# Moving two one-hot builds ahead of the block statistics on VectorE, and the square root behind a copy on ScalarE, in a one-core graph layer

## The chip, the cores and the metric

The kernel runs on one core of one Trainium2 chip. The metric is the device time of one launch in microseconds: the median of three runs before the change is 260.56 us (260.49 to 260.68).

## The reference

One layer of a graph network over 12,500 nodes (128 features) and 412,500 edges (48 features), sorted by destination node:

```python
h = jnp.maximum(_layernorm(x, axis=-1), 0.0)              # 12500 x 128
agg = jax.ops.segment_sum(edges, recv, num_segments=N)    # edges 412500 x 48, recv = dst, sorted
u = graph_globals[batch]                                  # batch is all zero: one row of 64
z = jnp.concatenate([h, agg, u], axis=1)                  # 240 wide
out = x + relu(z @ W1 + b1) @ W2 + b2                     # hidden width 256
```

Everything is float32.

## The kernel before

The nodes are taken in 12 turns of 1024, counted from 0 here (and a rest of 212 in an epilogue). A turn has two blocks, A and B, of 512 nodes, and 33,792 edges in 11 groups of 3072. The groups lie in six slots: `SLOTS = [(1, 6), (2, 7), (3, 8), (4, 9), (5,), (10, 11)]`; slot 4 holds one group, the others two. The edges of a group come by one DMA of 576 KB; block A and block B of x come by one DMA of 256 KB each. The outputs of the first 11 turns are held on chip (`hold`) and stored after the loop.

What a turn does, by engine. Each engine has its own instruction stream, in the order in which `body(it)` lists the calls, which is written out by hand; `Flow` only derives the semaphore waits from what each step reads and writes.

- **TensorE**, in this order. The sums of the six slots (`su0` to `su5`, L801): edges times one-hot matrices, which add the edges of each short run of nodes. The placing of the sums into the node columns (`place`, L823, and `place_ends`, L785, called `pc5` in the list of steps): sums times wider one-hots ("windows", L751). Second layer of block A of the turn before (`w20`, L907, 16 matmuls), most of the second layer of B (`w21a`, L901), transposes of the normalised blocks (`tu0`, `tu1`, L866), the rest of B's second layer, and the first layer (L876 on the normalised x, L881 on the placed sums).
- **VectorE**. Statistics of block A (`stats`, L831), two small steps (`farthest`, L692 and L694), the fetch of the destination offsets of the next turn (`fetch`, L730, writes `rel_i`), statistics of block B (L831), four small steps to the variance (`variance`, L836 to L841), the one-hot of slot 0 for the next turn (`onehots`, L745), the reciprocal and the shift (`shift`, L850 and L851), the one-hots of slots 1, 2 and 3, the output of block A (`second`, L911, `holda`, from `w20`'s result), the next `xb` of A (L861), one-hots of slots 4 and 5, the same two steps for block B, and the windows.
- **ScalarE**. A copy of each slot's sums out of PSUM (`ss0` to `ss5`, L805), the square root (`root`, L845), the normalisation of the two blocks, four activations each (`norm`, L857; it needs the shift), copies of the placed sums (L872), issue of the DMA that loads the next block A (behind L861 of A), copies of the transposes (L867), issue of the DMA that loads the next block B (behind L861 of B), and the four activations of the first layer (L886).
- **SyncE** issues the edge loads; a group's buffer is loaded again when its slot's sums are done.

Three dependences across engines matter here. `pc5` works in pairs: its first matmul takes the ends kept from the turn before (`ssf`), its second takes `ss5`, and only the weight load of the second waits for ScalarE's copy `ss5` (`late={"ss5": 1}`). L911 `holda` waits for the last matmul of `w20`, which stands right behind `pc5` on TensorE. The one-hot of a slot may be overwritten when this turn's sums of that slot are done, and it reads `rel_i`, which L730 has just written on the same engine.

In `Flow.run`, TensorE's share of a turn has a stretch that is skipped in the first turn (`f.brief = ("w20", "w21a")`). Its branch blocks are named `brief`, `whole` and `both`.

Of the kernel before, what the change touches and what calls it, by code (L numbers as in the profile page):

```python
# [54 lines left out]
class Flow:  # L55
# [14 lines left out]
    def op(self, eng, name, reads, writes, emit, dma=False, late=None):  # L70
        self.seq.append(dict(eng=eng, name=name, r=tuple(reads), w=tuple(writes), emit=emit, dma=dma, it=self.at, late=late or {}))
# [119 lines left out]
    def run(self):  # L191
# [22 lines left out]
        def ahead(e, late=False):  # L214
            for n, c in sorted(self.ahead[e].items()):
                if (e == "PE" and n in self.weights) == late:
                    self.of[e].wait_ge(self.sem[n], (self.rank[n, c] + self.extra[n]) * self.unit(n))

        def repeat(o, i):
            waits = []  # L220
            for n, back in self.body.get(o["name"], []):
                u = self.unit(n)
                waits.append((n, self.sem[n], regs[(o["eng"], u, (self.at_lo[n] - lo - back + self.extra[n]) * u)]))
            self.emit(o, waits, i)
# [26 lines left out]
        pe = nc.tensor  # L251
        blocks = {}

        def part(name, over, come=True):

            if come:
                pe.br("pe_" + name)
            blocks[name] = nc.switch_bb("pe_" + name, parent=over and blocks[over])

        def either(under, yes, no):  # L260

            pe.br_lt(j, under, on_true="pe_" + yes, on_false="pe_" + no)

        n = 4
# [35 lines left out]
        at = "first"  # L300
        for brief, some in groupby(own[:cut], lambda o: o["name"] in self.brief):
            some = list(some)
            if not brief:
                for o in some:
                    if o["name"] in self.stops:
                        stop = "at_" + o["name"]
                        at = "go_" + o["name"]
                        above, under, to = over[stop]
                        part(stop, above)
                        either(under, to, at)  # L310
                        part(at, stop, False)
                    repeat(o, None)
                continue
            either(n + 1, "brief", "whole")
            part("brief", at, False)
            ahead("PE", True)
            for o in some:
                if o["name"] in self.sem:
                    pe.sem_inc(self.sem[o["name"]], 1)
            pe.br("pe_both")  # L320
            part("whole", at, False)
            for o in some:
                repeat(o, None)
            part("both", at)
        pe.br("pe_head")
        part("after", "gate2", False)
        self.straight(end)
# [151 lines left out]
def kernel(  # L479
# [112 lines left out]
    A, B, Z = 0, 1, 2  # L592
# [22 lines left out]
    def load_e(s, j, only=None):  # L615

        for k, g in enumerate(SLOTS[s]):
            if only not in (None, k):
                continue
            dma("SP", f"le{s}.{k}", [], [f"e{s}.{k}"], e[s][:, k * CG:(k + 1) * CG],  # L620
                lambda i, g=g: span(edge_attr, i, lambda i: (i + j) % NIT * IE + g * GE, GE).rearrange("(c p t) d -> p c (t d)", p=P, t=T))
# [68 lines left out]
    def farthest():  # L690

        op("DVE", "fa", ["rel_i"], ["far"], lambda i: [nc.vector.tensor_reduce(  # L692
            far, rel_i.rearrange("p g t -> p (g t)"), AX.X, OP.max, apply_absolute_value=True)])
        op("DVE", "fm", ["far"], ["farm"], lambda i: [nc.vector.tensor_tensor(farm, farm, far, OP.max)])  # L694
# [26 lines left out]
    def fetch(j):  # L721

        it = (f.at or 0) + j
        g0, g1 = it * GI + 1, min(NG, (it + 1) * GI + 1)
        m = GI * CG
        blocks = [b for b in range(NB) if b * P < g1 * CG and (b + 1) * P > g0 * CG]
        rv = rel_i.rearrange("p g (c t) -> p (g c) t", t=T)
        at = lambda i: ((i + j) * GI + 1) * CG

        op("DVE", "fr", ["relz"] + [f"rel{b}.{t0}" for b in blocks for t0 in (0, 3)], ["rel_i"], lambda i: [nc.vector.tensor_scalar(  # L730
            rv, (rel[:, :, at(i):at(i) + m] if isinstance(i, int) else rel[:, :, ds(at(i), m)]).rearrange("p t c -> p c t"),
            0.0, None, OP.add)])
# [8 lines left out]
    def onehot(name, o, reads, r):  # L741

        k, n = r.shape[1], r.shape[2]
        ov = o.rearrange("p (k n) v -> p k n v", k=k)
        op("DVE", f"oh{name}", reads + ["iota_v"], [f"oh{name}"], lambda i: [nc.vector.tensor_tensor(  # L745
            ov, iota_v[:, None, None, :].to_broadcast([P, k, n, V]), r[:, :, :, None].to_broadcast([P, k, n, V]), OP.is_equal)])
# [6 lines left out]
    def onehots(s):  # L753
        g = SLOTS[s]
        onehot(s, oh[s], ["rel_i"], rel_i[:, g[0] - 1:g[0]] if len(g) == 1 else rel_i[:, g[0] - 1:g[1]:g[1] - g[0]])
# [32 lines left out]
    def keep_ends():  # L788
        op("ACT", "ssf", ["ss5"], ["ssf"], lambda i: [nc.scalar.copy(ssf, ss[5])])
# [17 lines left out]
    def sums(s):  # L807
        m = len(SLOTS[s])
        add_up(s, s % 2, oh[s], e[s], ss[s], [f"e{s}.{j}" for j in range(m)], m * CG, {1: (10, 36), 2: (36,)}.get(s, ()))
# [19 lines left out]
    def stats(k, m=P):  # L829
        c = k % 2 * R  # L830
        op("DVE", f"st{k}", [f"x{k}", f"x{k}t"], [f"st{k}"], lambda i: [nc.vector.bn_stats(st[k // 2][:m, c + r], xt[k][:m, r]) for r in range(RR[k])])  # L831

    def variance(n, ks, m=P):
        s, v = sm[n][:m], st[n][:m]
        op("DVE", f"sm{n}.0", [f"st{k}" for k in ks], [f"sm{n}a"], lambda i: [
            nc.vector.tensor_tensor(s[:, 0:2], v[:, :, 1:3].rearrange("p r c -> p c r"), v[:, :, 4:6].rearrange("p r c -> p c r"), OP.add)])  # L836
        op("DVE", f"sm{n}.1", [f"st{k}" for k in ks], [f"sm{n}b"], lambda i: [
            nc.vector.tensor_tensor(s[:, 2], v[:, :, 1], v[:, :, 4], OP.subtract)])
        f.chain("DVE", f"sm{n}.2", [f"sm{n}a"], [f"sm{n}b"],
            lambda: nc.vector.tensor_tensor(s[:, 2], s[:, 2], s[:, 2], OP.mult),  # L840
            lambda: nc.vector.scalar_tensor_tensor(s[:, 3], s[:, 2], D / 4.0, s[:, 1], OP.mult, OP.add))  # L841

    def root(n, m=P):
        op("ACT", f"sq{n}", [f"sm{n}b", "eps"], [f"sc{n}"], lambda i: [
            nc.scalar.activation(sc[n][:m], sm[n][:m, 3], AF.Sqrt, bias=eps[:m], scale=1.0 / D)])  # L845
# [7 lines left out]
    def norm(k, some, m=P):  # L853
        n, c = k // 2, k % 2 * R
        for r in some:
            op("ACT", f"xn{k}.{r}", [f"x{k}", f"x{k}t", f"sc{n}", f"sh{n}"], [f"xn{k}"], lambda i, r=r: [
                nc.scalar.activation(xn[k][:m, r], xt[k][:m, r], AF.Relu, bias=sh[n][:m, c + r:c + r + 1], scale=sc[n][:m, c + r:c + r + 1])])  # L857
# [145 lines left out]
    def body(it):  # L1003
        f.at = it

        def add_slots(*some):
            for s in some:
                sums(s)
                if it < NIT - 1:
                    load_e(s, 1)  # L1010

        keep = lambda i: (i + NIT - 2) % (NIT - 1)
        add_slots(0, 1)
        stats(A)
        farthest()
        fetch(1)
        add_slots(2)
        stats(B)
        variance(0, (A, B))
        root(0)  # L1020
        onehots(0)
        add_slots(3)
        shift(0)
        norm(A, (0,))
        add_slots(4)
        norm(A, (1, 2))
        onehots(1)
        add_slots(5)
        norm(A, (3,))
        norm(B, range(R))  # L1030
        onehots(2)
        onehots(3)
        place(0, (0, 1))
        for s in (1, 2, 3, 4):
            place(s)
        place_ends((0, 1))
        second(A, P, ph[A], "PH0", keep)
        add_b(A)
        for s in (4, 5):
            onehots(s)  # L1040
        second_begun(B, ph[B], "PH1", R - 1)
        sums_out(A)
        sums_out(B)
        if it < NIT - 1:
            load_x(A, lambda i: (i + 1) % NIT * IN)
        turn(A)
        turn(B, P, po, "PO")
        second(B, P, ph[B], "PH1", keep, R - 1)
        add_b(B)
        keep_ends()  # L1050
        if it < NIT - 1:
            load_x(B, lambda i: (i + 1) % NIT * IN + BN)
        places_far()
        fetch_off(1)
        for s in (0, 1, 2, 3, 4):
            places(s)
        places_near()
        layers(layer_x)
        layers(layer_e)
        layers(relu)  # L1060
# [93 lines left out]
```

## Time and profile before

| | us |
|---|---|
| median of 3 runs | 260.56 |
| the profiled execution | 260.67 |
| span of its trace, first to last instruction | 258.9 |
| TensorE matmul busy | 238.8 (92%) |
| VectorE busy | 230.8 (89%) |
| ScalarE busy | 127.9 (49%) |
| HBM rate over the span | 364 GB/s |

Times in the trace are counted from the start of the span. The first turns run while the pipeline of loads fills; the sums of turn 2 start at 62.34 us and those of the last turn at 224.92 us, so that a turn takes about 18.06 us. In a row of the timeline the first number is the start, the second the duration; "x3" merges three instructions, and a bracket tells how long the engine was idle before and what ended it. Rows of the chain of waits and of the list of waits name an engine, the tile that it writes and the line.

### The profile page before, as it was taken

What the parts mean: (1) busy time and instruction counts of PE and PEld (TensorE: products, weight loads), DVE (VectorE), ACT (ScalarE), POOL (GpSimd) and SP (SyncE); (2) the same over time, 40 slices, a digit from 0 to 9 for tenths busy, and PEclk for the clock granted to TensorE, in tenths of its full rate; (3) what the DMA queues carried; (4) which work ended last, traced back from release to release, by engine and by line L of the source; (5) the groups of instructions that cost most, each with busy time, mean ns of one, the idle gap of its engine ahead of it and who ended that gap; (6) DMA issues with size and microseconds to landing.
All of it is one profiled execution on the core that took longest, in us unless ns stands there. A gap on an engine that the chain in (4) does not pass through costs nothing.

```text
span 258.9 us, 17101 instructions
## 1 busy us (share of the span) xinstructions
PE 238.8 (92%) x7539; PEld 188.7 (73%) x7540; DVE 230.8 (89%) x572; ACT 127.9 (49%) x315; POOL 5.2 (2%) x18
## 2 busy tenths in 40 slices
PE   1866699899999999999999999999999999999990
PEld 1766565885976968949949869779589499598680
DVE  6699998978998998998998989989989989989740
ACT  5510273553644725725835646447257358355520
POOL 5000000000000000000000000000000000002000
PEclk9967579999999999999999999999999999999999
DMA  6999999999999999999999999999999999969951
GB/s 189 339 385 388 364 387 392 390 390 393 377 392 389 389 392 387 390 392 384 390 394 385 390 393 386 392 386 385 391 383 390 391 389 390 394 230 363 366 208 65
DMA packets 79508, 94.33 MB, mean 364 GB/s; under 512 B 3227, under 2 KB 72797, under 8 KB 79494
## 3 DMA queue, kind: packets, MB, share of 16 engines
q1 hardware_dynamic: 76086, 88.06, 95.5%
q10 hardware_dynamic: 3312, 6.03, 6.1%
q8 instruction: 7, 0.11, 0.2%
q0 software_dynamic: 96, 0.07, 0.1%
q14 instruction: 7, 0.06, 0.1%
HBM read 87.75 MB, written 6.40 MB: 364 GB/s over the span
## 4 chain that ended last, share of the span: by engine, by line
PE 78%; SPq 14%; DMA 4%; issue 1%; DVE 0%
PE s L801 23%; SPq L597 14%; PE ph L907 12%; PE ph L876 7%; PE ax L823 6%; PE ph L901 6%; PE pt L881 4%; PE pt L876 4%; DMA e<-in_edge_attr_dram 4%; PE ph L881 4%; PE po L876 4%; PE pt L866 2%; PE po L866 2%; PE ax L785 1%; PE ay L785 1%
## 5 line engine op out<-in xcount | busy, mean ns | idle before, releaser
L745 DVE TENSOR_TENSOR oh<-iota_v,rel_i 128x1344 f32<-128x1344 f32 (+1 forms) x78 | 108.7, 1435 | 0.0
L801 PEld LDWEIGHTS s<-e,oh 128*28 128x28 f32 x6336 | 74.2, 111 | 16.8 <-issue 14.5
L801 PE MATMUL s<-e,oh 128*28 128x48 f32 x6336 | 76.9, 212 | 7.4 <-issue 3.5
L886 ACT ACTIVATE hida<-pt,bias 128x512 f32<-128x512 f32 x12 | 8.2, 687 | 50.2 <-PE pt L881 50.2
L857 ACT ACTIVATE xna<-xa,shab,scab 128x128 f32<-128x128 f32 x48 | 23.7, 493 | 13.0 <-DVE shab L851 12.6
L805 ACT COPY ss<-s 128x96 f32<-128x96 f32 (+1 forms) x72 | 16.5, 229 | 26.5 <-PE s L801 25.7
L751 DVE TENSOR_SCALAR pl<-iota_w,off_i 128x186 f32<-128x186 f32 x117 | 27.6, 311 | 0.4
L907 PE MATMUL ph<-w,hida 128*128 128x128 f32 x192 | 24.6, 281 | 0.0
L857 ACT ACTIVATE xnb<-xb,shab,scab 128x128 f32<-128x128 f32 x48 | 23.5, 490 | 1.2
L907 PEld LDWEIGHTS ph<-w,hida 128*128 128x128 f32 x192 | 22.3, 191 | 0.6
L823 PE MATMUL ay<-pl,ss 128*48 128x186 f32 (+1 forms) x120 | 20.9, 324 | 0.0
L823 PE MATMUL ax<-pl,ss 128*48 128x186 f32 (+1 forms) x120 | 20.9, 324 | 0.0
L823 PEld LDWEIGHTS ax<-pl,ss 128*48 128x48 f32 x120 | 14.5, 129 | 4.1
L831 DVE BATCH_NORM_STATS2 stab<-xb 128x6 f32<-128x128 f32 x48 | 10.5, 282 | 6.9 <-DMA xb<-in_x_dram 6.9
L901 PE MATMUL ph<-w,hidb 128*128 128x128 f32 x132 | 16.5, 275 | 0.0
L901 PEld LDWEIGHTS ph<-w,hidb 128*128 128x128 f32 x132 | 15.6, 192 | 0.0
L823 PEld LDWEIGHTS ay<-pl,ss 128*48 128x48 f32 x120 | 14.5, 129 | 0.0
L876 PE MATMUL pt<-hta,w1h 128*128 128x512 f32 x24 | 13.5, 643 | 0.4 <-ACT hta L867 0.4
L881 PE MATMUL po<-ags,w1a 48*128 48x512 f32 x24 | 13.5, 641 | 0.0
L881 PE MATMUL pt<-ags,w1a 48*128 48x512 f32 x24 | 13.5, 641 | 0.0
L867 ACT COPY hta<-pt 128x512 f32<-128x512 f32 x12 | 7.0, 586 | 12.2 <-PE pt L866 12.2
L881 PE MATMUL ph<-ags,w1a 48*128 48x512 f32 x48 | 12.3, 589 | 0.0
(151 smaller groups left out, 330.3 us busy)
## 6 DMA issues: line engine op xcount, KB each, us to landing
e<-in_edge_attr_dram SPq DMA_DIRECT2D x133, 576.0 KB, 8.7
xa<-in_x_dram ACTq DMA_DIRECT2D x11, 256.0 KB, 5.4
xb<-in_x_dram ACTq DMA_DIRECT2D x11, 256.0 KB, 5.4
out_dram<-holda SPq DMA_DIRECT2D x11, 256.0 KB, 3.1
out_dram<-holdb SPq DMA_DIRECT2D x11, 256.0 KB, 3.1
holda<-in_dst_dram SPq DMA_DIRECT2D x4, 384.0 KB, 5.6
e<-in_edge_attr_dram SPq DMA_DIRECT2D x1, 720.0 KB, 4.7
xa<-in_x_dram SPq DMA_DIRECT2D x1, 256.0 KB, 6.6
```

The costliest lines, as they stand in the source:

```text
L597: return [f.of[eng].dma_start(dst_ap(i) if callable(dst_ap) else dst_ap, src_ap(i) if callable(src_ap) else src_ap)]
L745: op("DVE", f"oh{name}", reads + ["iota_v"], [f"oh{name}"], lambda i: [nc.vector.tensor_tensor(ov, iota_v[:, None, None, :].to_broadcast([ ...
L751: nc.vector.tensor_scalar(out[:, j], iota_w, o[j], None, OP.is_equal) for j in range(len(o))])
L801: nc.tensor.matmul(S[k][NV * c:NV * c + V, j * DE:(j + 1) * DE], o[:, (j * CG + c) * T + t], ev[:, j * CG + c, t * DE:(t + 1) * DE], start ...
L805: op("ACT", f"ss{name}", [f"S{k}"], [f"ss{name}"], lambda i: [nc.scalar.copy(sv.rearrange("p j d -> p (j d)"), S[k][:, :m * DE])])
L823: out.append(nc.tensor.matmul(agg[bk][h:h + DE, at:at + w], sv[:, j], pv[:, j, frm:frm + w], start=bk in fresh and bk not in seen, stop=Tr ...
L831: op("DVE", f"st{k}", [f"x{k}", f"x{k}t"], [f"st{k}"], lambda i: [nc.vector.bn_stats(st[k // 2][:m, c + r], xt[k][:m, r]) for r in range(R ...
L857: nc.scalar.activation(xn[k][:m, r], xt[k][:m, r], AF.Relu, bias=sh[n][:m, c + r:c + r + 1], scale=sc[n][:m, c + r:c + r + 1])])
L876: nc.tensor.matmul(o, w1h[:, a * P:(a + 1) * P], hT[k][:, :, :m], start=first, stop=False, skip_group_check=True)])
L881: nc.tensor.matmul(o, w1a[h:h + DE, a * P:(a + 1) * P], ag[k // 2][h:h + DE, :, :m], start=False, stop=True, skip_group_check=True)])
L901: nc.tensor.matmul(ov[:, r], hid[k][:, a, r], w2[:, a], start=(a == 0), stop=(a == NH - 1)) for r in range(n) for a in range(NH)])
L907: nc.tensor.matmul(ov[:m, r], hid[k][:, a, r, :m], w2[:, a], start=(a == 0), stop=(a == NH - 1)) for r in range(begun, RR[k]) for a in ran ...
```

## The change

VectorE builds the one-hot of slot 0 right behind the fetch, ahead of block B's statistics, and that of slot 1 right behind the variance, ahead of the shift. On ScalarE the square root moves behind the copy of slot 3; the first activation of block A moves behind the copy of slot 4, so that in front of the copy of slot 5 there are two activations of block A (three before) and behind it two (one before). TensorE's and SyncE's orders are the same. In `Flow.run` the names of the branch blocks get the name of the step that begins the stretch, so that there could be more than one such stretch; `f.brief` is not changed, and its two steps stand next to each other.

```diff
--- before.py
+++ after.py
@@ -311,17 +311,20 @@
-            either(n + 1, "brief", "whole")
-            part("brief", at, False)
-            ahead("PE", True)
+            tag = some[0]["name"]
+            either(n + 1, "brief_" + tag, "whole_" + tag)
+            part("brief_" + tag, at, False)
+            if tag == self.brief[0]:
+                ahead("PE", True)
...
-            pe.br("pe_both")
-            part("whole", at, False)
+            pe.br("pe_both_" + tag)
+            part("whole_" + tag, at, False)
             for o in some:
                 repeat(o, None)
-            part("both", at)
+            part("both_" + tag, at)
+            at = "both_" + tag
@@ -1014,19 +1017,18 @@
         stats(A)
         farthest()
         fetch(1)
+        onehots(0)
         add_slots(2)
         stats(B)
         variance(0, (A, B))
+        onehots(1)
+        add_slots(3)
         root(0)
-        onehots(0)
-        add_slots(3)
         shift(0)
-        norm(A, (0,))
         add_slots(4)
-        norm(A, (1, 2))
-        onehots(1)
+        norm(A, (0, 1))
         add_slots(5)
-        norm(A, (3,))
+        norm(A, (2, 3))
         norm(B, range(R))
         onehots(2)
         onehots(3)
```

## The prediction

> **What bounds the kernel now.** I read the stretches of single turns first, then the list of waits over turns 2 to 11, then the timelines of VectorE, ScalarE and TensorE side by side in one turn. One turn as a stretch (columns: TensorE, its weight loads, VectorE, ScalarE, GpSimd, then granted clock, DMA share and GB/s), two rows of the list of waits from 60 to 235 us, and the load of block B among the page's DMA issues:
>
> ```profile
> 200.98:219.06 18.08, 18.08 (x614) 14.20 (x614) 17.14 (x43) 9.77 (x25) 0.00 (x0) 1.00 1.08 391
> ```
> ```profile
> DVE stab L831 <- DMA xb<-in_x_dram: 6.2, 10, 0.7
> ACT xna L857 <- DVE shab L851: 11.0, 10, 1.1
> ```
> ```profile
> xb<-in_x_dram ACTq DMA_DIRECT2D x11, 256.0 KB, 5.4
> ```
>
> TensorE looks full (its ends are modelled), the DMA engines look full, and VectorE works 17.14 of 18.08 us. The list names one regular hole of VectorE, 0.6 us per turn for block B of x (5.4 us from issue to landing), and one of ScalarE, 1.1 us for the shift. So I followed turn 2, VectorE first:
>
> ```profile
> 54.26 0.69 DVE L911 TENSOR_TENSOR holda<-ph,xba 128x512 f32 x1 [1.65 <-PE ph L907]
> 58.55 0.69 DVE L861 TENSOR_TENSOR xbb<-xb,b_sb 128x512 f32<-128x512 f32 x1
> ...
> 63.62 0.41 DVE L730 TENSOR_SCALAR rel_i<-rel 128x264 f32 x1
> 64.74 0.87 DVE L831 BATCH_NORM_STATS2 stab<-xb 128x6 f32<-128x128 f32 x4 [0.71 <-DMA xb<-in_x_dram]
> ...
> 66.15 0.17 DVE L841 SCALAR_TENSOR_TENSOR smab<-smab 128x8 f32<-128x8 f32 x1
> 66.24 1.55 DVE L745 TENSOR_TENSOR oh<-iota_v,rel_i 128x1344 f32<-128x1344 f32 x1
> 67.70 0.20 DVE L850 RECIPROCAL scab<-scab 128x8 f32<-128x8 f32 x1
> 67.94 0.17 DVE L851 SCALAR_TENSOR_TENSOR shab<-smab,scab 128x8 f32<-128x8 f32 x1
> 68.02 4.49 DVE L745 TENSOR_TENSOR oh<-iota_v,rel_i 128x1344 f32<-128x1344 f32 x3
> 72.43 0.68 DVE L911 TENSOR_TENSOR holda<-ph,xba 128x512 f32 x1
> ```
>
> VectorE runs without a hole from the statistics of B at 64.74 to the last row and on to L861 of B. ScalarE in the same turn:
>
> ```profile
> 64.70 0.24 ACT L805 COPY ss<-s 128x96 f32<-128x96 f32 x1 [0.56 <-PE s L801]
> 65.73 0.24 ACT L805 COPY ss<-s 128x96 f32<-128x96 f32 x1 [0.79 <-PE s L801]
> 66.35 0.30 ACT L845 ACTIVATE scab<-smab,eps 128x8 f32<-128x8 f32 x1 [0.38 <-DVE smab L841]
> 66.75 0.24 ACT L805 COPY ss<-s 128x96 f32<-128x96 f32 x1
> 68.14 0.49 ACT L857 ACTIVATE xna<-xa,shab,scab 128x128 f32<-128x128 f32 x1 [1.15 <-DVE shab L851]
> 68.54 0.18 ACT L805 COPY ss<-s 128x48 f32<-128x48 f32 x1
> 68.67 1.02 ACT L857 ACTIVATE xna<-xa,shab,scab 128x128 f32<-128x128 f32 x2
> 69.59 0.22 ACT L805 COPY ss<-s 128x96 f32<-128x96 f32 x1
> ...
> 70.12 2.06 ACT L857 ACTIVATE xnb<-xb,shab,scab 128x128 f32<-128x128 f32 x4
> ```
>
> Third, TensorE's weight loads around `pc5`, in turn 1 and in turn 2, with the matmuls of `w20` behind them:
>
> ```profile
> 51.67 0.12 PEld L785 LDWEIGHTS ax<-plf,ssf 128*48 128x48 f32 x1
> 51.68 0.12 PEld L785 LDWEIGHTS ay<-pln,ss 128*48 128x48 f32 x1
> ```
> ```profile
> 69.62 0.20 PEld L785 LDWEIGHTS ax<-plf,ssf 128*48 128x48 f32 x2
> 69.86 0.12 PEld L785 LDWEIGHTS ay<-pln,ss 128*48 128x48 f32 x1
> ```
> ```profile
> 52.17 2.05 PE L907 MATMUL ph<-w,hida 128*128 128x128 f32 x16
> 70.32 2.05 PE L907 MATMUL ph<-w,hida 128*128 128x128 f32 x16
> ```
>
> In turn 1 the load that takes `ss5` follows 0.01 us behind its partner. In turn 2 it comes 0.24 us behind, 0.05 us after the copy `ss5` ends (69.59 + 0.22 = 69.81). No idle time is booked, because earlier matmuls are still drawn as running, but TensorE is held here. So the turn is not set by TensorE's work: it is set by a ring of steps. The shift ends at 68.11; three activations and a copy lie between it and the end of `ss5`; `w20` ends 2.56 us behind `ss5` (70.32 + 2.05 = 72.37); VectorE comes to `holda` at 72.43, 0.06 us behind `w20`. Both ways from the shift to `holda` are equally long, and the ring closes through L861 of B, which ends at 59.24, its load (5.4 us) and the statistics at 64.74.
>
> **The change part by part: the ring with the new order.** I start from `holda` and walk to the next `holda`.
>
> (a) `holda` to the fetch L730: 63.62 − 54.26 = 9.36 us, all of it VectorE's own work, as before. (b) The one-hot of slot 0 now follows the fetch and reads what it wrote. The trace has that pair in the prologue:
>
> ```profile
> 12.94 0.38 DVE L730 TENSOR_SCALAR rel_i<-rel 128x264 f32<-128x264 f32 x1
> 13.35 3.03 DVE L745 TENSOR_TENSOR oh<-iota_v,rel_i 128x1344 f32<-128x1344 f32 x2
> ```
>
> It starts 0.03 us after the fetch ends; with the loop's 0.41 us that is 0.44 us. Its other condition, that the sums of slot 0 are done, holds by then: `ss1` waits for its sums until 64.70 and `ss2` until 65.73, so a slot takes 1.03 us and slot 0 is done by about 63.67; the one-hot starts at 64.06. (c) One-hot of slot 0 to the statistics of B: 1.47 us, the spacing of the row of three, (4.49 − 1.55) / 2. Block B has landed: in the old order it did so at 64.74, and the statistics now begin at 65.53, so the hole of 0.71 us goes. (d) Statistics and variance to the next one-hot: 66.24 − 64.74 = 1.50 us. (e) One-hot of slot 1 to the reciprocal: 1.47 us; its buffer is free, since slot 1's sums end near 64.70 and it starts at 67.03. (f) Reciprocal to the end of the shift: 67.94 + 0.17 − 67.70 = 0.41 us.
>
> So the fetch to the shift's end takes 0.44 + 1.47 + 1.50 + 1.47 + 0.41 = 5.29 us, where it took 68.11 − 63.62 = 4.49 us. The hole paid for only half of the second one-hot: the shift comes 0.80 us later.
>
> The root stays hidden: the variance ends 66.15 + 0.17 − 64.74 = 1.58 us behind the start of B's statistics, so at 67.11, and the copy `ss3`, now ahead of the root, at 66.75 + 0.24 = 66.99; the root takes 0.30 us, and the reciprocal comes only at 68.50. If that cover were gone, up to 0.30 us would join the ring. The copy `ss4` (half a slot, so ready near 67.3) now stands ahead of the first activation and falls into the wait for the shift.
>
> (g) Shift to the first activation: 68.14 − 68.11 = 0.03 us. (h) First to second activation: 1.02 − 0.49 = 0.53 us. (i) Second activation to the copy `ss5`: 0.40 us, as from the activation at 68.14 to the copy at 68.54, and 0.22 us of copy. From the shift to the end of `ss5` that is 1.18 us, where it was 69.81 − 68.11 = 1.70. The edit on ScalarE gives back 0.52 us of the 0.80.
>
> (j) End of `ss5` to the end of `w20`: 2.56 us. (k) End of `w20` to `holda` when VectorE is waiting: 0.04 us, as in turn 1 (52.17 + 2.05 = 54.22 to 54.26). VectorE is waiting now: it has two one-hots behind the shift instead of three, so it is ready 4.32 − 1.47 = 2.85 us after the shift, and `w20` ends 1.18 + 2.56 = 3.74 us after it. The hole that was closed at the statistics opens again at `holda`, about 0.9 us wide.
>
> The ring: 9.36 + 5.29 + 1.18 + 2.56 + 0.04 = 18.43 us. The rows are rounded; 18.41 from the steadier ones (9.35 and 0.40 in the later turns). Before, from turn 2 to the last turn:
>
> ```profile
> 234.94 0.68 DVE L911 TENSOR_TENSOR holda<-ph,xba 128x512 f32 x1
> ```
>
> (234.94 − 72.43) / 9 = 18.06 us. So 0.35 us per turn for nine turns is 3.15. Turn 2 itself: 54.26 + 18.41 = 72.67 against 72.43, 0.24. Turns 0 and 1 keep their end, because the last sums of turn 1 wait for edges:
>
> ```profile
> 49.65 0.71 PE L801 MATMUL s<-e,oh 128*28 128x48 f32 x48 [0.70 <-DMA e<-in_edge_attr_dram]
> ```
>
> and `ss5` there, late or not, has until 51.68. The epilogue follows `w20` and is unchanged. The sum is +3.4 us on the profiled 260.67, which is 0.1 above the median: **264.0 us** (+1.3%).
>
> **Other edits.** The rows for what follows `w20` on TensorE and ScalarE (the copy at 56.16 is from turn 1, its label for the wait is in the row):
>
> ```profile
> 73.55 0.60 PE L866 MATMUL pt<-ident,xna 128*128 128x128 f32 x4
> ```
> ```profile
> 56.16 0.59 ACT L867 COPY hta<-pt 128x512 f32<-128x512 f32 x1 [2.07 <-PE pt L866]
> ...
> 72.66 0.58 ACT L872 COPY ags<-ay 48x512 f32<-48x512 f32 x1
> ```
>
> Moving the second activation of block A behind `ss5` costs nothing: all eight end as long after the shift as now (70.12 + 2.06 − 68.11 = 4.07 us), so 0.3 us after `w20`, and the transposes start 1.18 us after it (73.55 against 72.37). The copies of the placed sums, the last ending at 73.24 and right behind the activations now, then end about 1.4 us after `w20`; the copy of the transposes comes 56.16 − 54.22 = 1.94 us after it. No DMA is issued from another place; both loads of x hang on `holda` and keep their distance to it. Edge loads start with TensorE's sums, 0.35 us further apart. The renamed branch blocks are the same single stretch, two steps side by side, so nothing.
>
> **A rule against a row.** The row: a one-hot lasts 1.55 us and the next independent instruction starts 1.47 us after it (67.70 behind 66.24). The Trainium skill, page "VectorE: DVE Perf Modes", section "The DRAIN you can't avoid", says that the next operation does not start until the pipe is empty, and that a semaphore costs nothing extra. By that each of the two one-hots would cost 1.55, the ring would be 18.57 and the time about 265.6. The overlap of 0.08 us in this trace decides for 1.47.
>
> **The rivals.** *Faster: the closed hole is all.* Place: the copy `ss5`. Two activations stand ahead of it instead of three, so it gains 0.52 us on the shift; were the shift less than 0.45 us later (0.80 less the 0.35 of the sum), the turn would be shorter than 18.06. TensorE's 0.2 us of holding would go, and then the transfers would bound: 11 x 576 KB + 2 x 256 KB is 7.01 MB per turn, at the stretch's 391 GB/s 17.93 us, so 0.13 us for ten turns: 259.3. For it speaks the wait at 64.74; against it every VectorE row above, since a one-hot would have to cost 1.1 us.
>
> *No change: transfers set the turn.* The stretch shows 391 GB/s and a full DMA share; if loads set the 18.06, a later `ss5` is absorbed: 260.6. The Trainium skill, "Perfetto Trace Analysis", section "Identifying the Most-Contended Engine", points that way with its rule that the busiest resource is the one to work on. Against it: the list of waits from 60 to 235 us has no wait of TensorE for edges, and the weight load starts 0.05 us behind `ss5`.
>
> *Slower still: ScalarE's chain slips past the transposes.* The copy of the transposes comes 1.9 us after `w20`, and the work ahead of it ends at 1.4. With 0.5 us more delay than I count, each further tenth costs a tenth per turn; 0.3 past it is 267.
>
> **How the numbers follow.** The ring as worked out: 0.83; no change 0.08; faster 0.05; slower still 0.04. Inside the first case (b) is the least sure: if the one-hot overlaps the fetch by 0.09, as independent pairs do, it is 0.32, the ring 18.29 and the time 262.8; it is no longer than 0.44 by any pair here. Two one-hots that each keep the next instruction until 0.03 us past their end add 0.24 per turn, 266.4, but the rows of just such pairs overlap, so I stop at 265.3. With a little of the other cases below, 262.2 to 265.3. A measurement here tells about 0.2% (0.5 us) from no change. Slower 0.86, same 0.08, faster 0.06.
>
> **What the changed profile would show.** The statistics of B no longer wait for the load; L911 `holda` waits about 0.9 us for L907 in each turn from 2 on; ScalarE's wait for the shift grows to about 1.4 us; the weight load of `ss5` still starts 0.05 us behind the copy, now about 0.5 us behind its partner; `holda` recurs every 18.4 us; DMA falls to about 381 GB/s. I would be wrong if the period stays at 18.0, if `ss5` ends before TensorE needs it, or if the one-hot behind the fetch starts early.

## The result and the profile after

The changed kernel takes 264.67 us (median of 4 runs, 264.45 to 265.22); the kernel before took 260.62 us beside it. The ratio is 1.0154, with a 95% interval of 1.0130 to 1.0177: slower by 4.05 us. The profiled execution took 264.80 us, with a span of 263.0 us. In this kernel's rows the line numbers are higher by three: L748 is the one-hot, L834 the statistics, L914 `holda`, L808 the copy of the sums, L860 the normalisation, L788 `pc5`, L910 `w20`.

VectorE in turn 2, from `holda` to `holda`, and the last `holda`:

```profile
54.80 0.69 DVE L914 TENSOR_TENSOR holda<-ph,xba 128x512 f32 x1 [1.81 <-PE ph L910]
...
64.15 0.41 DVE L733 TENSOR_SCALAR rel_i<-rel 128x264 f32 x1
64.60 1.56 DVE L748 TENSOR_TENSOR oh<-iota_v,rel_i 128x1344 f32<-128x1344 f32 x1
66.07 0.87 DVE L834 BATCH_NORM_STATS2 stab<-xb 128x6 f32<-128x128 f32 x4
...
67.57 1.55 DVE L748 TENSOR_TENSOR oh<-iota_v,rel_i 128x1344 f32<-128x1344 f32 x1
69.03 0.20 DVE L853 RECIPROCAL scab<-scab 128x8 f32<-128x8 f32 x1
69.27 0.17 DVE L854 SCALAR_TENSOR_TENSOR shab<-smab,scab 128x8 f32<-128x8 f32 x1
69.35 3.02 DVE L748 TENSOR_TENSOR oh<-iota_v,rel_i 128x1344 f32<-128x1344 f32 x2
73.21 0.69 DVE L914 TENSOR_TENSOR holda<-ph,xba 128x512 f32 x1 [0.84 <-PE ph L910]
...
239.00 0.69 DVE L914 TENSOR_TENSOR holda<-ph,xba 128x512 f32 x1 [0.84 <-PE ph L910]
```

The bracket at the statistics of B is gone and a wider one stands at `holda`. ScalarE in the same turn, then TensorE's weight loads of `pc5` and its matmuls of `w20`:

```profile
67.30 0.24 ACT L808 COPY ss<-s 128x96 f32<-128x96 f32 x1 [0.78 <-PE s L804]
67.69 0.30 ACT L848 ACTIVATE scab<-smab,eps 128x8 f32<-128x8 f32 x1
67.89 0.18 ACT L808 COPY ss<-s 128x48 f32<-128x48 f32 x1
69.47 1.02 ACT L860 ACTIVATE xna<-xa,shab,scab 128x128 f32<-128x128 f32 x2 [1.39 <-DVE shab L854]
70.39 0.22 ACT L808 COPY ss<-s 128x96 f32<-128x96 f32 x1
...
75.05 0.59 ACT L870 COPY hta<-pt 128x512 f32<-128x512 f32 x1 [0.48 <-PE pt L869]
```
```profile
70.14 0.20 PEld L788 LDWEIGHTS ax<-plf,ssf 128*48 128x48 f32 x2
70.66 0.12 PEld L788 LDWEIGHTS ay<-pln,ss 128*48 128x48 f32 x1 [0.32 <-ACT ss L808]
```
```profile
71.12 2.05 PE L910 MATMUL ph<-w,hida 128*128 128x128 f32 x16
```

The weight load comes 0.05 us behind the end of `ss5` (70.61), as before, but 0.52 us behind its partner instead of 0.24. Between the two stands the second of the merged loads of `ax`; it ends at 70.34, and the 0.32 us behind it are booked as idle time of the weight loads. Before, it ended at 69.82 and the held load started at 69.86, so that nothing was booked. The same in the list of waits from 60 to 238 us, and one turn as a stretch:

```profile
ACT xna L860 <- DVE shab L854: 14.0, 10, 1.4
DVE holda L914 <- PE ph L910: 7.6, 9, 0.8
PEld ay L788 <- ACT ss L808: 4.0, 10, 0.4
```
```profile
202.16:220.58 18.42, 18.28 (x614) 14.20 (x613) 17.24 (x41) 9.82 (x25) 0.00 (x0) 1.00 1.07 380
```

The page's chain by engine, first of the kernel before, then of the changed one:

```profile
PE 78%; SPq 14%; DMA 4%; issue 1%; DVE 0%
```
```profile
DVE 45%; PE 24%; SPq 14%; issue 7%; ACT 4%; DMA 4%; DVEq 1%
```

Before, the chain went through TensorE in every turn, because no idle time was booked on it, although a ring through VectorE and a load set the turn (the run with ScalarE's edit alone, below, shows that). Once the waits are long enough to be booked, the chain goes round the ring.

### The profile page after: what moved, and what is told of

Its sections match the earlier page's. It is cut to its first block, busy times and chain, and to the rows that moved or that the text cites. A ratio compares the mean times of both kernels' runs of the same rounds, so it can differ in the third digit from the quotient of the medians.

```text
span 263.0 us, 17114 instructions
## 1 busy us (share of the span) xinstructions
PE 241.0 (92%) x7539; PEld 188.6 (72%) x7540; DVE 231.9 (88%) x572; ACT 128.6 (49%) x315; POOL 4.7 (2%) x18
## 4 chain that ended last, share of the span: by engine, by line
DVE 45%; PE 24%; SPq 14%; issue 7%; ACT 4%; DMA 4%; DVEq 1%
DVE oh L748 18%; SPq L600 14%; PE ph L910 10%; DVE pl L754 6%; DVE stab L834 5%; DMA e<-in_edge_attr_dram 4%; ACT xna L860 3%; PE s L804 3%; DVE holda L914 2%; DVE holdb L914 2%; PE ay L788 2%; DVE plf L767 2%; DVE rel_i L733 1%; PE ph L879 1%; DVE pln L767 1%
## 5 line engine op out<-in xcount | busy, mean ns | idle before, releaser
L748 DVE TENSOR_TENSOR oh<-iota_v,rel_i 128x1344 f32<-128x1344 f32 (+1 forms) x78 | 109.8, 1436 | 1.2 <-PE s L804 0.8
L808 ACT COPY ss<-s 128x96 f32<-128x96 f32 (+1 forms) x72 | 16.5, 229 | 37.1 <-PE s L804 37.0
L860 ACT ACTIVATE xna<-xa,shab,scab 128x128 f32<-128x128 f32 x48 | 23.7, 494 | 17.3 <-DVE shab L854 16.5
L910 PE MATMUL ph<-w,hida 128*128 128x128 f32 x192 | 24.6, 281 | 0.0
L860 ACT ACTIVATE xnb<-xb,shab,scab 128x128 f32<-128x128 f32 x48 | 23.5, 489 | 1.2
L910 PEld LDWEIGHTS ph<-w,hida 128*128 128x128 f32 x192 | 22.3, 191 | 0.6
L914 DVE TENSOR_TENSOR holda<-ph,xba 128x512 f32 x12 | 8.3, 692 | 10.4 <-PE ph L910 10.2
L879 PE MATMUL ph<-htb,w1h 128*128 128x512 f32 x24 | 12.3, 592 | 0.0
```

The costliest lines, as they stand in the source:

```text
L808: op("ACT", f"ss{name}", [f"S{k}"], [f"ss{name}"], lambda i: [nc.scalar.copy(sv.rearrange("p j d -> p (j d)"), S[k][:, :m * DE])])
L879: nc.tensor.matmul(o, w1h[:, a * P:(a + 1) * P], hT[k][:, :, :m], start=first, stop=False, skip_group_check=True)])
L910: nc.tensor.matmul(ov[:m, r], hid[k][:, a, r, :m], w2[:, a], start=(a == 0), stop=(a == NH - 1)) for r in range(begun, RR[k]) for a in ran ...
L914: op("DVE", f"ho{k}", [key, f"xb{k}"] + (["spare"] if k == A else []), [f"hold{k}.{keep(f.at)}"], lambda i: [nc.vector.tensor_tensor(cols( ...
```

## The experiments

Each is the kernel before with another order in `body`, so its line numbers are those of before; two diffs are shorter against the changed kernel and say so in their first line. Times are medians; ratios are against the kernel before on the same chip.

**Slot 0's one-hot alone.**

```diff
         fetch(1)
+        onehots(0)
         add_slots(2)
...
         root(0)
-        onehots(0)
         add_slots(3)
```

> Only slot 0's one-hot moves, to behind the fetch; slot 1's stays behind the shift and ScalarE keeps its old order. Ring theory: the load of block B is hidden (the statistics start 11.3 us after holda, the load lands after 10.5), the root is now bare and costs VectorE about 0.38 us, so holda to holda is 9.35 + 0.44 + 1.47 + 1.58 + 0.38 + 0.41 + 4.32 = 17.95 us against 18.06: about 1 us less, 259.5. Rival, one-hots ahead of the shift are what costs: half of the change's loss, 262.6. Rival, transfers set the turn: 260.6.

Measured 265.24 us, ratio 1.0169 (1.0149 to 1.0190), `holda` every 18.49 us. Neither the ring's 259.5 nor either rival's time came. VectorE's part came as worked out (the reciprocal waits 0.37 us for the root), but something else holds TensorE. Two `holda`, ScalarE's rows, TensorE's sums, and two rows of the list of waits:

```profile
110.46 0.69 DVE L911 TENSOR_TENSOR holda<-ph,xba 128x512 f32 x1 [0.46 <-PE ph L907]
128.95 0.69 DVE L911 TENSOR_TENSOR holda<-ph,xba 128x512 f32 x1 [0.46 <-PE ph L907]
```
```profile
123.35 0.30 ACT L845 ACTIVATE scab<-smab,eps 128x8 f32<-128x8 f32 x1 [1.23 <-DVE smab L841]
123.56 0.22 ACT L805 COPY ss<-s 128x96 f32<-128x96 f32 x1
```
```profile
118.48 4.87 PE L801 MATMUL s<-e,oh 128*28 128x48 f32 x432
123.83 1.22 PE L801 MATMUL s<-e,oh 128*28 128x48 f32 x96 [0.48 <-ACT ss L805]
```
```profile
PEld s L801 <- ACT ss L805: 6.0, 10, 0.6
PE s L801 <- ACT ss L805: 4.6, 10, 0.5
```

In the old order on ScalarE the root stands ahead of the copy `ss3`. The root now waits longer for the variance, because VectorE makes a one-hot first; `ss3` stands behind it; and the sums of slot 5 write the PSUM buffer that `ss3` empties (the kernel has two such buffers and gives them to the slots in turn, `S[s % 2]`). The expectation had counted the root's wait on VectorE alone and not what is queued behind the root on ScalarE.

**That reason, split in two.** Slot 0's one-hot as above, with one half of ScalarE's edit each: first the root behind `ss3`, then only the two-and-two split of the activations.

```diff
+        add_slots(3)
         root(0)
-        add_slots(3)
         shift(0)
```

> Slot 0's one-hot behind the fetch and of ScalarE's edit only the root behind the copy ss3; the activations keep their old order. New theory: with slot 0's one-hot alone the root stood ahead of ss3 and waited for a later variance; ss3 left late, and the sums of slot 5, which use the same PSUM bank, held TensorE 0.5 us per turn. With the root behind ss3 that goes: VectorE's ring 17.95 and the ring through ss5 9.35 + 4.28 + 1.70 + 2.56 + 0.04 = 17.93: 259.5. Rival, the order of the activations around ss5 was the cause: 265.2.

```diff
         shift(0)
-        norm(A, (0,))
         add_slots(4)
-        norm(A, (1, 2))
+        norm(A, (0, 1))
         onehots(1)
         add_slots(5)
-        norm(A, (3,))
+        norm(A, (2, 3))
```

> Slot 0's one-hot behind the fetch and of ScalarE's edit only the activations (two ahead of ss5, two behind); the root stays ahead of ss3. New theory: ss3 is still late and slot 5's sums still wait 0.5 us: 18.48 us per turn, 265.2. Rival, the order of the activations around ss5 was the cause: 259.5.

With the root behind `ss3`: 259.53 us, ratio 0.9958 (0.9939 to 0.9977), `holda` every 17.95 us. With the root ahead: 264.94 us, 1.0157 (1.0128 to 1.0186), every 18.49 us, and the same two rows of TensorE's wait for `ss3`. These two runs differ in the split as well, but with slot 0's one-hot alone (265.24 us: root ahead, old split) and the run further down with both halves (259.54) all four combinations are there. By the medians, which come from different chips, the root's place is worth 5.7 us with the old split and 5.4 with the new one; the split is worth 0.3 us with the root ahead, less than the spread of those runs, and nothing with the root behind. `holda`, first with the root behind, then ahead:

```profile
107.96 0.68 DVE L911 TENSOR_TENSOR holda<-ph,xba 128x512 f32 x1
125.91 0.68 DVE L911 TENSOR_TENSOR holda<-ph,xba 128x512 f32 x1
```
```profile
110.20 0.69 DVE L911 TENSOR_TENSOR holda<-ph,xba 128x512 f32 x1 [0.46 <-PE ph L907]
128.69 0.69 DVE L911 TENSOR_TENSOR holda<-ph,xba 128x512 f32 x1 [0.46 <-PE ph L907]
```

**Slot 1's one-hot alone**, ahead of the shift, with slot 0's left ahead of it and ScalarE as before.

```diff
         variance(0, (A, B))
-        root(0)
         onehots(0)
+        onehots(1)
+        root(0)
         add_slots(3)
...
-        onehots(1)
         add_slots(5)
```

> Only slot 1's one-hot moves, to ahead of the shift; slot 0's stays behind the variance, ScalarE keeps its old order. Ring theory: the wait for block B's load stays (10.48 us after holda), then 1.50 + 2.94 + 0.41 to the shift, 1.70 to the end of ss5, 2.56 to the end of w20, 0.04 to holda: 19.63 us, 1.57 more per turn, about 276. Rival, the change's loss is shared by the two one-hots: 262.6.

Measured 274.86 us, ratio 1.0549 (1.0524 to 1.0574), every 19.43 us against 19.63 expected. The ring is right, its term for the load was too long:

```profile
132.34 0.69 DVE L911 TENSOR_TENSOR holda<-ph,xba 128x512 f32 x1 [1.37 <-PE ph L907]
...
142.63 0.87 DVE L831 BATCH_NORM_STATS2 stab<-xb 128x6 f32<-128x128 f32 x4 [0.52 <-DMA xb<-in_x_dram]
...
151.76 0.69 DVE L911 TENSOR_TENSOR holda<-ph,xba 128x512 f32 x1 [1.36 <-PE ph L907]
```

From `holda` to the statistics it is 10.29 us instead of 10.48. The 10.48 was read from turn 2 of the kernel before; from turn 3 on the same stretch takes 10.33 to 10.40 us there. From 74 to 220 us this kernel moves 363 GB/s where the one before moves 389; whether the lighter traffic makes the few hundredths that are left is not shown.

**ScalarE's edit alone.**

```diff
         variance(0, (A, B))
+        add_slots(3)
         root(0)
         onehots(0)
-        add_slots(3)
         shift(0)
-        norm(A, (0,))
         add_slots(4)
-        norm(A, (1, 2))
+        norm(A, (0, 1))
...
-        norm(A, (3,))
+        norm(A, (2, 3))
```

> ScalarE's edit alone, VectorE as before. Ring theory: ss5 ends 0.52 us earlier and TensorE's hold at its weight load goes (the load follows its partner by under 0.1 us instead of 0.24), but VectorE's own ring through block B's load (12.65 us of work and 5.4 of load) still takes 18.05: 260.6, no change, the hole of 0.6 us stays. Rival, TensorE's hold was what set the turn: 17.9 us, 259.

Measured 260.82 us, ratio 0.9999 (0.9984 to 1.0015). TensorE's hold at `pc5` is gone and the turn is the same:

```profile
88.08 0.12 PEld L785 LDWEIGHTS ax<-plf,ssf 128*48 128x48 f32 x1
88.09 0.12 PEld L785 LDWEIGHTS ay<-pln,ss 128*48 128x48 f32 x1
```
```profile
DVE stab L831 <- DMA xb<-in_x_dram: 6.2, 10, 0.8
PEld pt L876 <- ACT hta L867: 2.2, 9, 0.4
```

A hold of up to 0.4 us now stands at the first layer, which waits for the copy of the transposes; before, that row is not in the list from 60 to 235 us. VectorE's ring through the load of B sets the turn: `holda` comes every 18.06 us, as before.

**VectorE's edit alone**, ScalarE as before.

```diff
         fetch(1)
+        onehots(0)
         add_slots(2)
         stats(B)
         variance(0, (A, B))
+        onehots(1)
         root(0)
-        onehots(0)
...
-        onehots(1)
         add_slots(5)
```

> VectorE's edit alone, ScalarE in its old order (three activations and ss4 between the shift and ss5). Ring theory: the 0.52 us that the edit on ScalarE gave back are missing, 18.41 + 0.52 = 18.93 us per turn, 5 us above the change: about 269.6. Rival, ScalarE's order does not matter: 264.7.

Measured 270.05 us, ratio 1.0363 (1.0338 to 1.0388), every 18.94 us, 0.52 more than in the changed kernel: the third activation ahead of `ss5`, as in the sum. The root stands ahead of `ss3` here too, and TensorE waits for `ss3` (0.5 us, nine times in the list), yet the turn is no longer than the ring through `ss5` makes it: the two holds do not add.

```profile
92.66 0.69 DVE L911 TENSOR_TENSOR holda<-ph,xba 128x512 f32 x1 [1.37 <-PE ph L907]
111.61 0.69 DVE L911 TENSOR_TENSOR holda<-ph,xba 128x512 f32 x1 [1.36 <-PE ph L907]
```

**The ring cut at `ss5`.** The changed order on VectorE, but all activations behind the copy `ss5`.

```diff
--- after.py
         add_slots(4)
-        norm(A, (0, 1))
         add_slots(5)
-        norm(A, (2, 3))
+        norm(A, range(R))
         norm(B, range(R))
```

> VectorE as in the change, but ScalarE copies ss5 ahead of all activations, so that it no longer stands behind the shift. Ring theory: pc5 and w20 no longer wait for the shift, VectorE alone needs 9.35 + 5.28 + 2.85 = 17.5 us, and the transfers 17.95; ScalarE's activations now end 0.8 us after w20 and may push the copy of the transposes by 0.3 us, which gives up to 18.1. So 259.6 to 261. Rival, the two one-hots ahead cost VectorE time as such: 264.7 as before.

Measured 259.19 us, ratio 0.9948 (0.9927 to 0.9969), every 17.92 us, a little under the 259.6 to 261 expected: the wait of the first layer for the copy of the transposes (`hta`), which was to give up to 18.1, is not in its list. The same two one-hots in the same two places cost nothing once `ss5` does not stand behind the shift, so it is not VectorE's time that the change lost:

```profile
126.35 0.69 DVE L911 TENSOR_TENSOR holda<-ph,xba 128x512 f32 x1 [0.30 <-PE ph L907]
...
144.28 0.69 DVE L911 TENSOR_TENSOR holda<-ph,xba 128x512 f32 x1 [0.35 <-PE ph L907]
```
```profile
126.35:144.28 17.93, 17.93 (x614) 14.05 (x613) 17.24 (x42) 10.07 (x25) 0.00 (x0) 1.00 1.08 391
```

**The change without slot 1's one-hot.**

```diff
--- after.py
         variance(0, (A, B))
-        onehots(1)
         add_slots(3)
...
         norm(A, (0, 1))
+        onehots(1)
         add_slots(5)
```

> Slot 0's one-hot behind the fetch and the whole edit on ScalarE; only slot 1's one-hot stays behind the shift. Ring theory: VectorE's ring is 17.95 us as with slot 0's one-hot alone, ss5 is no longer late, TensorE is not held: about 259.5, the fastest here. Rival, ss5 was still the limit with slot 0 alone: then this one is a further 1 us or more below it.

Measured 259.54 us, ratio 0.9955 (0.9939 to 0.9971), every 17.95 us. It is 5.7 us below slot 0's one-hot alone, as the rival asked, but not for the rival's reason: with the root behind `ss3` and the old split, which leaves three activations ahead of `ss5`, it is 259.53 us. "The fastest here" is not shown, since the intervals of the three orders near 259.5 overlap. VectorE has no wait left but the bare root:

```profile
121.94 0.20 DVE L850 RECIPROCAL scab<-scab 128x8 f32<-128x8 f32 x1 [0.37 <-ACT scab L845]
```

**Both kernels again**, for the start of the loop.

> The changed kernel once more, unchanged. In its first profile holda of turn 1 stood at 54.80 us against 54.26. If the edit causes that (the prologue's loads are the same, so I doubt it), it is 54.8 again and before's is 54.3 again; if it is a difference of loads from run to run, the two kernels overlap. Time 264.6, holda every 18.42 us.

> The kernel before once more, unchanged, for the same question: holda of turn 1 between 54.2 and 54.9 us, its period 18.06, time 260.6.

The changed kernel took 264.34 us (ratio 1.0151, 1.0119 to 1.0182), the one before 260.38 (one run). The changed kernel's `holda` in turn 1, and that of the kernel before:

```profile
54.03 0.69 DVE L914 TENSOR_TENSOR holda<-ph,xba 128x512 f32 x1 [0.84 <-PE ph L910]
```
```profile
54.06 0.69 DVE L911 TENSOR_TENSOR holda<-ph,xba 128x512 f32 x1
```

With the first profiles that is 54.80 and 54.03 for the changed kernel, 54.26 and 54.06 for the one before: the two kernels overlap, and no effect of the edit on the start is shown. The four starts lie in the order in which SyncE came to issue the load of the first layer's weights: 22.46 and 23.61 us for the changed kernel at 54.03 and 54.80, 22.88 and 22.91 for the one before at 54.06 and 54.26.

## Why the prediction was right

**The ring with the new order.** Its terms against turn 2 after: (a) 64.15 − 54.80 = 9.35 us (9.36 said), (b) 64.60 − 64.15 = 0.45 (0.44 said), (c) 1.47 (1.47), (d) 1.50 (1.50), (e) 1.46 (1.47), (f) 69.44 − 69.03 = 0.41 (0.41); shift to the end of `ss5` 70.61 − 69.44 = 1.17 (1.18); (j) 73.17 − 70.61 = 2.56 (2.56); (k) 0.04 (0.04). The turn is 73.21 − 54.80 = 18.41 us (18.41 said), and 18.42 for the mean of the ten. The runs that take the ring apart agree: one more activation ahead of `ss5` adds 0.52 us per turn, and without the link from the shift to `ss5` the loss is gone.

**The size.** 4.05 us were measured, 3.4 said, 264.67 against 264.0. From `holda` of turn 1 to that of turn 11 it is 239.00 − 54.80 = 184.20 us against 180.68 before: 3.52 of the 4.13 us between the two profiled executions, for 3.15 + 0.24 = 3.39 in the sum. Another 0.54 is the later start of turn 1, for which the prediction had no term ("Turns 0 and 1 keep their end"). In the second pair the starts agree (54.03 and 54.06), that stretch grew by 3.71 us, and the profiled executions are 264.00 − 260.38 = 3.62 us apart. So the ring's term was short by 0.1 to 0.3 us, and the rest of the first pair's difference is the start. That the start spreads in the runs without a trace as well is likely, and not shown.

**The waits.** The hole at the statistics closed and opened again at `holda`, as said: 0.84 us for "about 0.9". ScalarE's wait for the shift is 1.39 us ("about 1.4"), the weight load 0.52 us behind its partner ("about 0.5"), the traffic 380 GB/s in a turn ("about 381").

**The rule against the row.** The next independent instruction starts 1.47 us behind the one-hot at 64.60, which lasts 1.56. The row held, and the 265.6 us worked out without an overlap is further off. The Trainium skill, page "VectorE: DVE Perf Modes", section "The DRAIN you can't avoid", says behind the sentence that the prediction used that a next operation which is not held starts earlier. The trace agrees with that, 1.47 against 1.56 us; the prediction had read the first half alone, so page and row were no rivals.

**The rivals.** *Transfers set the turn* is refuted: the turn grew and the rate fell to 380 GB/s. *The closed hole is all* names the case that comes about when the shift is not late, or when `ss5` does not wait for it: 259.54 and 259.19 us, for 259.3 worked out. *ScalarE slips past the transposes* did not come: the copy of the transposes at 75.05 still waits 0.48 us for TensorE.

**A step that was priced wrongly, without harm here.** The prediction said of the root that it stays hidden and that losing its cover would put up to 0.30 us into the ring. It saw only VectorE's wait, which is 0.37 us in the runs with slot 0's one-hot. Those runs show a second price, through `ss3` and slot 5's PSUM buffer: 5.4 to 5.7 us for the launch by the root's place alone. In the changed kernel the root stands behind `ss3`, so the sum did not meet that price; the prediction had not reckoned with it, and that it did no harm is luck. In the changed order it would have been small: from the end of the variance to `holda` it is 128.95 − 123.32 = 5.63 us in the run with slot 0's one-hot alone and 73.21 − 67.65 = 5.56 us in the changed kernel, which is about 0.1 us per turn (an estimate from these rows; no run has that order).

**What sets the faster orders.** The trace has the time at which each edge load landed. The last group of a turn lands closest to its use; in the kernel before and in the three faster orders it lands on average 17.94 us after that of the turn before. In the kernel before, it is there 0.04 us ahead of its first matmul in turn 2 and 1.11 us ahead in turn 11, so the transfers did not set the 18.06 us. With the root behind `ss3` it lands 0.04 to 0.05 us ahead in each of the turns 2 to 9, and 0.04 is also what is left where a wait for edges is booked; VectorE has no hole there but the root's 0.37 us. So transfers and VectorE's ring both take about 17.95 us, and this run cannot tell which of them sets the turn. With the copy first it lands 0.29 us ahead in turn 2 and 0.04 in turn 11, and VectorE waits 0.3 us at `holda`: neither sets the 17.92 us there until the last turn, which leaves the chain through TensorE. How much of that chain is TensorE's own work stays open. The three orders at 259.2 to 259.5 us are faster than both kernels; their intervals overlap, so they are not ranked.

## What to carry to other kernels

Before filling a hole on an engine, walk the ring that the hole belongs to and ask what stands behind the step that the filler delays: here one more one-hot of 1.5 us was put ahead of the shift for the sake of a hole of 0.7 us, and a copy in another engine's queue carried the lateness to TensorE. An instruction that waits is priced by all that is queued behind it on its engine: with the same one-hots moved, the square root behind one copy, or the last copy ahead of the activations, was worth 0.5 us per turn, where filling the hole brought 0.1. Where two paths end within 0.1 us of each other, as at `holda` before, do not expect much from freeing one of them: ScalarE's edit alone freed the path through `ss5` and brought nothing.

## What the runs showed of the hardware that was not expected

A hold of TensorE of about 0.2 us left no idle time in the records: before, the weight load stood 0.24 us behind its partner without a row in the list of waits, and the chain gave TensorE 78%. Another weight load stood between the two (it ended at 69.82, the held one started at 69.86), and the matmuls in front are drawn as running until 70.10. In the same way TensorE can be held by edges without a row: with the root behind `ss3` the last group lands 0.04 to 0.05 us ahead of its first matmul in eight turns running, which follows the matmul ahead of it by 0.04 to 0.07 us instead of 0.02, and the list names no wait for edges.
